# Two attention layers on one core: VectorE in written order for the first two attentions, and a last chunk with its own sums

## The chip, the cores and the metric

The kernel runs on one core of one Trainium2 chip. Its time is the device time of one execution in microseconds (us). Before the change the median of 9 runs is 3087.87 us (3086.91 to 3088.94). A profile of one execution stands beside it; this execution itself took 3088.43 us.

The engines of a core work side by side, each through its own list of instructions in order: TensorE (PE) multiplies matrices into PSUM, VectorE (DVE) and ScalarE (ACT) work on elements, GpSimd (POOL) does little here, and SyncE (SP) issues most DMAs. Semaphores order work between engines.

## The reference

The input `x` has 8 images of 64 channels and 64 x 64 positions (n = 4096). Two layers follow one another:

```python
# layer 0, for each image
f, g, hh = Wf @ x + bf, Wg @ x + bg, Wh @ x + bh     # 8, 8 and 64 channels
beta = softmax(f^T @ g)                              # 4096 x 4096
x = x + hh @ beta^T
# layer 1, for each image
xn = group_norm(x, 8 groups) * gamma + beta
q, k, v = split(w_qkv @ xn + b_qkv)                  # 64 channels each
o = softmax(q^T @ k / 8) @ v
out = x + w_proj @ o + b_proj
```

All of it is in float32.

## The kernel before

**Layout.** An image lies on 128 partitions: 64 channels times two halves of its positions, 2048 columns each. An attention is cut into NC = 4 chunks of 512 query columns per half (1024 queries), and a chunk into NT = 16 steps of keys. A step gives one tile `e` of 128 x 2048 float32, exponentials of scores for 256 keys and 1024 queries. There are six buffers of `e` (pool `ppool`, line 101).

**A step.** TensorE makes scores in PSUM banks, ScalarE writes their exponentials to `e` (line 877 for layer 0, line 836 for layer 1), TensorE multiplies `e` with the values and adds this up in a bank (`weigh`), and VectorE adds `e` to the running sum `esum` (line 749), which becomes the denominator of the softmax. There is no maximum subtracted; instead a flag `n_bad` counts sums outside a range, and if it isn't zero a general path (lines 894 on) does all again. With these inputs the general path does not run.

**Banks.** Of eight PSUM banks, 0 and 7 hold the weighted sums (`outer`), the six between are three pairs that `pair()` hands out in turn (`turn`, lines 110 to 120). In layer 0 a group of scores takes six or seven banks, and a projection borrows a pair (`lent`).

**End of a chunk.** `finish` (line 327) copies the weighted sum to `raw`, folds `esum`, and gives three pieces of work that are done some steps later: `sums` (products with ones, a copy to `zs`, four small DMAs to `zt`), `reciprocals` (a reciprocal into `stash` on 8 columns, then a DMA to DRAM and two that broadcast it to `r`) and `result` (multiply, residual). The very last chunk has a function of its own, `end` (line 379): it adds up the sums on VectorE, turns them to columns by eight products, takes the reciprocal on 128 x 8, tests the bounds, spreads the reciprocals by a diagonal matrix `diag` and two products, and writes the output over two queues.

**Order of the attentions.** It is layer 0 of image 0, layer 0 of image 1, layer 1 of image 0, layer 0 of image 2, layer 1 of image 1, and so on (lines 669 to 672). So only at the start do two attentions of layer 0 follow each other. While the second runs, the group norm and the projections of layer 1 of image 0 are made: `channels` (aggregate of the statistics), `means`, `deviations` (an inverse square root by four Newton rounds, 16 small operations) and `normal` (which makes `xn`), lines 552 to 614. In the same way the projections of the next attention of layer 0 (`project`, line 488: `full` on ScalarE, then `high` and its split on VectorE, then 16 DMAs) are made in steps of the one before.

**What sets the order.** Each piece of work is put down for a step with `at_step` and taken by `take` (line 685) in the loop over steps, between scores and weighing. The matmuls are chained in the order in which they are written (`in_order`, line 124, and `matmul`). The instructions of VectorE and ScalarE are not: a scheduler places them by its own estimate, and `issue_after` only holds some of them back. VectorE's list in the built program is therefore not the written one; small operations lie between the running sums.

Of the kernel before, what the change touches and what calls it, by code (L numbers as in the profile page):

```python
# [19 lines left out]
CW = 512  # L20
# [12 lines left out]
@with_exitstack  # L33
def kernel(
    ctx: ExitStack,
    tc: tile.TileContext,
    x: bass.AP,
    WfT: bass.AP,
    bf: bass.AP,
    WgT: bass.AP,  # L40
    bg: bass.AP,
    WhT: bass.AP,
    bh: bass.AP,
    gamma: bass.AP,
    beta: bass.AP,
    WqkvT: bass.AP,
    bqkv: bass.AP,
    WpT: bass.AP,
    bp: bass.AP,
    out: bass.AP,  # L50
):

    nc = tc.nc
    args = (x, WfT, bf, WgT, bg, WhT, bh, gamma, beta, WqkvT, bqkv, WpT, bp, out)
    flag = ctx.enter_context(tc.tile_pool(name="flag", bufs=1))  # L60
    n_bad = flag.tile([1, 1], I32, name="n_bad")
    fast_path(tc, n_bad, *args)
    reg = nc.values_load(n_bad[0:1, 0:1], min_val=0, max_val=2 * P)
    with tc.If(reg > 0):
        general_path(tc, *args)
# [3 lines left out]
def fast_path(  # L69
# [42 lines left out]
    turn = 0  # L112
# [9 lines left out]
    tensor_last = None  # L122

    def in_order(made):

        nonlocal tensor_last
        if tensor_last is not None:
            tc.add_manual_dep(
                made.ins,
                tensor_last.name,  # L130
                mybir.DependencyInfo(mybir.DependencyClass.NoSync, mybir.DependencyReason.DATA),
                reason="order",
            )
        tensor_last = made.ins
# [165 lines left out]
    class Attention:  # L300
# [8 lines left out]
        def values(self, src, w, c):  # L309
# [11 lines left out]
            copy = nc.vector.tensor_copy if lent is None or first_ else nc.scalar.copy  # L321
# [5 lines left out]
        def finish(self, acc, esum, c, index):  # L327
# [6 lines left out]
            with tc.issue_after(copied.ins if self.kind == 1 else added):  # L334
                nc.vector.tensor_add(esum[:, 0], esum[:, 0], esum[:, 1])  # L335
# [27 lines left out]
            def reciprocals():  # L363
                rt = stash[:, ts(index, QP)]
                nc.vector.reciprocal(rt, zt)
# [7 lines left out]
            def result():  # L373
                nc.vector.tensor_mul(raw, raw, r)  # L374
                self.residual(raw, c)
# [3 lines left out]
        def end(self, acc, esum, e, t):  # L379


            c = NC - 1
            total = esum[:, 0]
            with tc.issue_after(added):
                for part in (esum[:, 1], e[:, 0], e[:, 1]):
                    nc.vector.tensor_add(total, total, part)  # L386
            z, laid = pair()[:, 0, 0:QP], pair()[:, 0, :]
            parts = [(h, k) for h in range(2) for k in range(TPC)]
            for p in range(2):
                self.weigh(acc, e[:, p], t, p, False, p == 1, slice(0, CW))  # L390
            for i, (h, k) in enumerate(parts):
                matmul(
                    z[:, i : i + 1], total[:, h, ts(k, P)], ones[:, 0:1], start=True, stop=True
                )
            rt = small.tile([P, QP], F32, tag="zt", bufs=4, name="rt")
            nc.vector.reciprocal(rt, z)
            bounds(rt, 1)
            raw = work.tile([P, CW], F32, tag="raw", bufs=4, name="raw_end")
            diag = work.tile([P, QP, P], F32, tag="full", bufs=1, name="diag")
            for h in range(2):  # L400
                nc.vector.tensor_mul(  # L401
                    diag[:, ts(h, TPC), :],
                    ident.unsqueeze(1).broadcast_to([P, TPC, P]),
                    rt[:, ts(h, TPC)].unsqueeze(2).broadcast_to([P, TPC, P]),
                )
            self.total(raw, acc)
            for i in range(2):
                matmul(bad_ps, bad[:, i : i + 1], ones[:, 0:1], start=i == 0, stop=i == 1)
            nc.vector.tensor_copy(n_bad, bad_ps)
            for h in range(2):  # L410
                matmul(
                    laid[ts(h, C), :], ones, diag[:, ts(h, TPC), :].rearrange("q k n -> q (k n)"),
                    start=True, stop=True,
                )
            nc.vector.tensor_mul(raw, raw, laid)
            self.residual(raw, c, (nc.sync, nc.scalar))

    class Layer0(Attention):
# [51 lines left out]
        def project_direct(self):  # L470
# [4 lines left out]
            for i, dst in enumerate((self.f, self.g)):  # L475
# [6 lines left out]
                nc.vector.tensor_copy(high[:, i, :], full[:, i, :])  # L482
                nc.vector.scalar_tensor_tensor(
# [4 lines left out]
        def project(self, k, js=(0, 1)):  # L488
# [14 lines left out]
            nc.vector.tensor_copy(high[rows], full[rows])  # L503

            split = high
            self.split = nc.vector.scalar_tensor_tensor(  # L506
# [31 lines left out]
        def residual(self, o, c):  # L538
            xc = x_tiles[self.b][:, ts(c, CW)]
            nc.vector.scalar_tensor_tensor(xc, o, hb, xc, op0=ALU.add, op1=ALU.add)  # L540
            nc.vector.bn_stats(self.st[:, c, :], xc)

    class Layer1(Attention):
# [8 lines left out]
        def before(self):  # L552
# [7 lines left out]
            def channels():  # L560
                nc.vector.bn_aggr(mv, self.st())

            def means():
# [5 lines left out]
                nc.vector.tensor_sub(d, mv[:, 0:1], mu)  # L569
                nc.vector.scalar_tensor_tensor(v, d, d, mv[:, 1:2], op0=ALU.mult, op1=ALU.add)  # L570

            def deviations():
# [4 lines left out]
                nc.vector.tensor_scalar_add(ve, ve, EPS)  # L577

                guess = small.tile([P, 1], I32, tag="guess", name=f"guess_{n}")
                nc.vector.tensor_single_scalar(  # L580
                    guess, ve.bitcast(I32), 1, op=ALU.logical_shift_right
                )
                nc.vector.tensor_scalar(
# [4 lines left out]
                for i in range(4):  # L588
                    nc.vector.scalar_tensor_tensor(w, y, y, ve, op0=ALU.mult, op1=ALU.mult)  # L589
                    nc.vector.tensor_scalar(w, w, -0.5, 1.5, op0=ALU.mult, op1=ALU.add)  # L590
                    nc.vector.tensor_mul(y, y, w)
                nc.vector.tensor_mul(self.a, y, k1["gam"])

            def normal(c):
                xns[c] = work.tile([P, CW], F32, tag="xn", bufs=1, name=f"xn_{n}_{c}")
                nc.vector.tensor_scalar(  # L596
# [8 lines left out]
            at = [18, 21, 24] if self.b == 0 else [16, 20, 24]  # L605
            units = [(at[0], channels, False), (at[1], means, True), (at[2], deviations, True)]
            for c in range(NC):
                s = 30 + 8 * c
                units += [
                    (s - 3, lambda c=c: normal(c), False),  # L610
# [42 lines left out]
        def total(self, raw, acc):  # L653
            nc.vector.tensor_copy(raw, acc[0])  # L654
            return nc.vector.tensor_add(raw, acc[1], raw)

        def residual(self, o, c, queues=(nc.sync, nc.sync)):
            nc.vector.scalar_tensor_tensor(
                o, o, k1["pb"], x_tiles[self.b][:, ts(c, CW)], op0=ALU.add, op1=ALU.add
            )  # L660
            for h in range(2):
                queues[h].dma_start(out[self.b, :, ds(h * NH + c * CW, CW)], o[ts(h, C), :])
# [71 lines left out]
    def weigh(i, j, e, cols, now):  # L734
# [12 lines left out]
        else:  # L747
            with tc.issue_after(layers0[0].split.ins) if i == 0 and t == 1 else nullcontext():
                added = nc.vector.tensor_add(esum, first if t == 1 else esum, e).ins  # L749
# [56 lines left out]
    bad = const.tile([P, 2], F32, name="bad")  # L806
    bad_ps = banks[0:1, 0, 0:1]

    def bounds(recip, i):
        ok = work.tile(list(recip.shape), F32, tag="raw", bufs=4, name=f"ok_{i}")  # L810
        nc.vector.tensor_scalar(ok, recip, 1.0 / SUM_MAX, None, op0=ALU.is_ge)
        nc.vector.scalar_tensor_tensor(
            ok, recip, 1.0 / SUM_MIN, ok, op0=ALU.is_le, op1=ALU.mult
        )
        least = small.tile([P, 1], F32, tag="least", name=f"least_{i}")
        nc.vector.tensor_reduce(least, ok, axis=AX.X, op=ALU.min)
        nc.vector.tensor_scalar(bad[:, i : i + 1], least, -1.0, 1.0, op0=ALU.mult, op1=ALU.add)

    at_step(len(seq) * NT - 3, lambda: bounds(stash, 0), 0)

    i = 0
    while i < len(seq):
        at, c = seq[i]
        if at.kind == 1:
# [64 lines left out]
    assert not later  # L889
    seq[-1][0].end(acc, esum, ready[0][2], NT - 1)  # L890
# [387 lines left out]
```

## Time and profile before

| | us |
|---|---|
| median of 9 runs | 3087.87 |
| the profiled execution | 3088.43 |
| its span, first to last instruction | 3086.7 |
| TensorE busy | 3051.4 (99%) |
| VectorE busy | 2534.8 (82%) |
| ScalarE busy | 2043.7 (66%) |
| mean granted TensorE clock | 0.995 |
| one running sum (line 749), 895 of them | 2.291 each, 2050.2 in all |

A line of a group or of the timeline names the source line, the engine, the operation, the tile written, the tile read and their shapes; in brackets stands how long the engine was idle just before and what ended this idle time. A line of waits has the total in us, how often, and the longest. A line of windows has the stretch, its length, and then the busy time of TensorE, its weight loads, VectorE, ScalarE and GpSimd with their number of instructions, and after them the granted TensorE clock (1.00 is full speed), the share of busy DMA engines and GB/s. A float32 matmul stands in the trace as two records, so the counts of matmuls there are twice those of the code.

### The profile page before, as it was taken

How to read it: one execution, taken by the hardware profiler on the slowest of the kernel's cores; microseconds unless marked ns; L12 is line 12 of the kernel's file. 1: busy time of each engine (PE TensorE's matmuls, PEld its weight loads, DVE VectorE, ACT ScalarE, POOL GpSimd, SP SyncE). 2: the span in 40 equal slices, each digit the busy share in tenths (PEclk: the TensorE clock that was granted, in tenths of full speed). 3: DMA queues.
4: the chain of work that ended last, by engine and by line, in shares of the span. 5: the costliest groups of instructions: out<-in, count | busy, mean ns of one | idle time of the engine just before them, and what ended most of it. 6: DMA issues, size and time to landing. Idle time of an engine off the chain costs nothing.

```text
span 3086.7 us, 59407 instructions
## 1 busy us (share of the span) xinstructions
PE 3051.4 (99%) x26083; PEld 1134.3 (37%) x26083; DVE 2534.8 (82%) x1612; ACT 2043.7 (66%) x1999; POOL 16.9 (1%) x45
## 2 busy tenths in 40 slices
PE   8999999999999999999999999999999999999998
PEld 3333334333343333433334333343333433334433
DVE  7998877899768997689877898779987799876666
ACT  7877655786557865578655785558855588555554
POOL 2000000000000000000000000000000000000000
PEclk9999999999999999999999999999999999999999
DMA  3000010100101001010010100100001000000000
GB/s 78 22 8 11 18 39 15 32 1 15 39 18 29 1 15 39 22 25 1 15 39 22 25 1 18 41 21 22 1 26 35 19 8 1 15 22 15 9 15 12
DMA packets 57531, 62.54 MB, mean 20 GB/s; under 512 B 30816, under 2 KB 30864, under 8 KB 57264
## 3 DMA queue, kind: packets, MB, share of 16 engines
q1 hardware_dynamic: 56192, 58.38, 7.6%
q8 instruction: 206, 3.38, 0.5%
q14 instruction: 61, 0.50, 0.1%
q0 software_dynamic: 672, 0.12, 0.0%
q10 hardware_dynamic: 400, 0.17, 0.0%
HBM read 25.06 MB, written 8.65 MB: 11 GB/s over the span
## 4 chain that ended last, share of the span: by engine, by line
PE 93%; DVE 5%; issue 1%; ACT 1%; DMA 0%; SPq 0%; DVEq 0%; ACTq 0%
PE banks L137 93%; DVE esum_l L749 4%; ACT e_l L836 0%; ACT e_l L877 0%; DVE vt_l L322 0%; DVE esum_l L386 0%; DVE esum_l L335 0%; DMA x<-in_x_dram 0%; ACT full_l L501 0%; DVE x L540 0%; DVE raw_l L374 0%; SPq L166 0%; DVE high_l L506 0%; DVE diag L401 0%; DVE w_l L589 0%
## 5 line engine op out<-in xcount | busy, mean ns | idle before, releaser
L749 DVE TENSOR_TENSOR esum_l<-esum_l,e_l 128x2048 f32<-128x2048 f32 x895 | 2050.2, 2291 | 461.7 <-ACT e_l L836 403.6
L836 ACT ACTIVATE e_l<-banks 128x1024 f32<-128x1024 f32 x1024 | 992.9, 1022 | 800.1 <-PE banks L137 776.7
L137 PE MATMUL banks<-e_l,v_l 64*64 64x512 f32 (+2 forms) x8772 | 1104.1, 589 | 0.0
L877 ACT ACTIVATE e_l<-banks 128x2048 f32<-128x2048 f32 (+3 forms) x765 | 956.2, 1314 | 196.9 <-PE banks L137 189.8
L137 PE MATMUL banks<-kq_l 64*64 64x512 f32 (+1 forms) x8448 | 1009.8, 586 | 2.6 <-ACT e_l L877 1.3
L137 PE MATMUL banks<-e_l,vt_l 128*64 128x512 f32 (+1 forms) x4060 | 831.9, 550 | 0.0
L137 PEld LDWEIGHTS banks<-e_l,v_l 64*64 64x64 f32 (+1 forms) x8772 | 363.0, 134 | 577.1 <-issue 530.2
L137 PEld LDWEIGHTS banks<-kq_l 64*64 64x64 f32 (+1 forms) x8448 | 348.0, 135 | 577.9 <-issue 546.6
L137 PEld LDWEIGHTS banks<-e_l,vt_l 128*64 128x64 f32 x4060 | 266.9, 136 | 471.4 <-issue 451.3
L137 PE MATMUL banks<-fg_l 32*128 32x512 f32 x1792 | 209.4, 459 | 4.8 <-ACT e_l L877 3.2
L749 DVE TENSOR_TENSOR esum_l<-e_l,e_l 128x2048 f32<-128x2048 f32 x64 | 146.4, 2287 | 11.5 <-ACT e_l L836 9.4
L137 PEld LDWEIGHTS banks<-fg_l 32*128 32x128 f32 x1792 | 85.3, 182 | 187.2 <-ACT e_l L877 138.3
L335 DVE TENSOR_TENSOR esum_l<-esum_l 128x1024 f32<-128x1024 f32 x63 | 76.8, 1219 | 0.8
L654 DVE COPY raw_l<-banks 128x512 f32<-128x512 f32 x31 | 21.4, 691 | 31.3 <-PE banks L137 31.3
L628 ACT ACTIVATE kq_l<-banks,qkb 128x512 f32<-128x512 f32 x64 | 40.7, 697 | 4.0 <-PE banks L137 4.0
L374 DVE TENSOR_TENSOR raw_l<-raw_l,r_l 128x512 f32<-128x512 f32 x63 | 43.1, 684 | 0.0
L137 PE MATMUL banks<-esum_l,ones 128*32 128x256 f32 x504 | 40.3, 391 | 1.6 <-DVE vt_l L322 1.6
L137 PE MATMUL banks<-xn_l,wqk 64*64 64x512 f32 x256 | 34.3, 607 | 4.1 <-DVE xn_l L596 4.1
L137 PEld LDWEIGHTS banks<-wh,x 64*64 64x64 f32 x1024 | 23.1, 138 | 15.3 <-issue 14.2
L137 PEld LDWEIGHTS banks<-wvp,xn_l 64*64 64x64 f32 x1024 | 20.6, 134 | 16.8 <-issue 16.8
L536 ACT COPY raw_l<-banks 128x512 f32<-128x512 f32 x32 | 19.0, 593 | 11.6 <-PE banks L137 11.4
L540 DVE SCALAR_TENSOR_TENSOR x<-raw_l,hb,x 128x512 f32<-128x512 f32 x32 | 24.0, 751 | 1.1
(108 smaller groups left out, 392.0 us busy)
## 6 DMA issues: line engine op xcount, KB each, us to landing
r_l<-recips SPq DMA_DIRECT2D x126, 128.0 KB, 2.9
fg_l<-high_l SPq DMA_DIRECT2D x216, 64.0 KB, 2.0
kq_l<-kq_l SPq DMA_DIRECT2D x64, 128.0 KB, 2.3
out_dram<-raw_l SPq DMA_DIRECT2D x62, 128.0 KB, 2.4
x<-in_x_dram SPq DMA_DIRECT2D x30, 256.0 KB, 4.8
zt_l<-zs_l SPq DMA_DIRECT2D x252, 1.0 KB, 1.7
kq_l<-high_l SPq DMA_DIRECT2D x32, 64.0 KB, 2.0
recips<-stash SPq DMA_DIRECT2D x63, 4.0 KB, 1.4
```

Source lines behind the costliest of these rows:

```text
L137: in_order(nc.tensor.matmul(*args, **kwargs))
L335: nc.vector.tensor_add(esum[:, 0], esum[:, 0], esum[:, 1])
L374: nc.vector.tensor_mul(raw, raw, r)
L536: nc.scalar.copy(raw, acc[0])
L540: nc.vector.scalar_tensor_tensor(xc, o, hb, xc, op0=ALU.add, op1=ALU.add)
L628: nc.scalar.activation(self.parts[:, h, cols], ps[:, h, :], AF.Identity, bias=k1["qkb"][:, h : h + 1],)
L654: nc.vector.tensor_copy(raw, acc[0])
L749: added = nc.vector.tensor_add(esum, first if t == 1 else esum, e).ins
L836: nc.scalar.activation(e[:, p], both_ps[p], AF.Exp, scale=at.scale)
L877: nc.scalar.activation(e.rearrange("k p h n -> k (p h) n")[:, first_ : first_ + n_, :], banks[:, bank : bank + n_, :], AF.Exp, scale=at.scale,
```

## The change

- `in_order` now keeps a chain for each engine. All VectorE instructions of the fast path are made through `vector`, which adds them to VectorE's chain while `tight` is true: that is for the first two attentions (`i < 2 * NC`) and for `end`. In the rest, and in the units before the first step, VectorE's order is left to the scheduler as before.
- The unit numbers of layer 1 of image 0 move: `means` from 21 to 22, `deviations` from 24 to 26, the projections from 30 + 8c to 31 + 8c; `normal` is 4 steps ahead of its projection instead of 3, so its step stays (for other images it is one earlier than before).
- `turn` starts at 2 instead of 0.
- An `issue_after` at the first running sum is gone.
- `end` is written anew: the sums come from products with ones of the two halves of `esum` and of the sum of both halves of the last `e`, 12 products into one bank; the reciprocal is taken there on all 128 partitions, 4 groups of 32 equal rows, 256 columns; four products of 32 rows with a column of `ident` spread it; `raw` is copied by ScalarE. The flag is apart: `zs` is copied by ScalarE, dealt to 128 x 8 by two products, tested in two operations, and nine products of one column add it up. Both output DMAs go on SP.

The core of the diff:

```diff
-    turn = 0
+    turn = 2
...
+    made_last = {}
+    tight = False
+
+    def in_order(made, engine="tensor"):
...
+    class InOrder:
+        def __getattr__(self, name):
+            def made(*args, **kwargs):
+                it = getattr(nc.vector, name)(*args, **kwargs)
+                if tight:
+                    in_order(it, "vector")
+                return it
+
+            return made
+
+    vector = InOrder()
...
         def end(self, acc, esum, e, t):
             c = NC - 1
-            total = esum[:, 0]
-            with tc.issue_after(added):
-                for part in (esum[:, 1], e[:, 0], e[:, 1]):
-                    nc.vector.tensor_add(total, total, part)
-            z, laid = pair()[:, 0, 0:QP], pair()[:, 0, :]
-            parts = [(h, k) for h in range(2) for k in range(TPC)]
+            width = CW // 2
+            parts = [(h, i) for h in range(2) for i in range(2)]
+            groups = [slice(32 * g, 32 * (g + 1)) for g in range(4)]
+            ps, laid = pair(), pair()[:, :, 0:width]
+            z, dealt = ps[:, 0, 0:width], ps[:, 1, 0:QP]
+            both_e = ppool.tile([P, 2, 2, CW], F32, tag="e", name="both_e")[:, 0]
+            for k, src in enumerate((esum[:, 0], esum[:, 1], both_e)):
+                if k == 2:
+                    vector.tensor_add(both_e, e[:, 0], e[:, 1])
+                for rows, (h, i) in zip(groups, parts):
+                    matmul(
+                        z[rows, :], ones[:, 0:32], src[:, h, ts(i, width)],
+                        start=k == 0, stop=k == 2, tile_position=(0, rows.start),
+                    )
             for p in range(2):
                 self.weigh(acc, e[:, p], t, p, False, p == 1, slice(0, CW))
-            for i, (h, k) in enumerate(parts):
-                matmul(
-                    z[:, i : i + 1], total[:, h, ts(k, P)], ones[:, 0:1], start=True, stop=True
-                )
-            rt = small.tile([P, QP], F32, tag="zt", bufs=4, name="rt")
-            nc.vector.reciprocal(rt, z)
-            bounds(rt, 1)
-            raw = work.tile([P, CW], F32, tag="raw", bufs=4, name="raw_end")
-            diag = work.tile([P, QP, P], F32, tag="full", bufs=1, name="diag")
-            for h in range(2):
-                nc.vector.tensor_mul(
-                    diag[:, ts(h, TPC), :],
...
-                )
-            self.total(raw, acc)
-            for i in range(2):
-                matmul(bad_ps, bad[:, i : i + 1], ones[:, 0:1], start=i == 0, stop=i == 1)
-            nc.vector.tensor_copy(n_bad, bad_ps)
-            for h in range(2):
-                matmul(
-                    laid[ts(h, C), :], ones, diag[:, ts(h, TPC), :].rearrange("q k n -> q (k n)"),
-                    start=True, stop=True,
-                )
-            nc.vector.tensor_mul(raw, raw, laid)
-            self.residual(raw, c, (nc.sync, nc.scalar))
+            rt = work.tile([P, width], F32, tag="zs", name="rt")
+            vector.reciprocal(rt, z)
+            zs = work.tile([P, width], F32, tag="zs", name="zs_end")
+            nc.scalar.copy(zs, z)
+            raw = work.tile([P, CW], F32, tag="raw", bufs=4, name="raw_end")
+            nc.scalar.copy(raw, acc[0])
+            vector.tensor_add(raw, acc[1], raw)
+            for rows, (h, i) in zip(groups, parts):
+                matmul(
+                    laid[ts(h, C), i, :],
+                    ident[rows, rows.start : rows.start + 1].broadcast_to([32, C]), rt[rows, :],
+                    start=True, stop=True, tile_position=(rows.start, h * C),
+                )
+            by_half = raw.rearrange("p (i n) -> p i n", i=2)
+            vector.tensor_mul(by_half, by_half, laid)
+            for k in range(2):
+                matmul(
+                    dealt[:, ts(k, 4)], zs[:, ts(k, P)], ident[:, 0:P:32], start=True, stop=True
+                )
+            ok = small.tile([P, QP], F32, tag="zt", bufs=4, name="ok_end")
+            vector.tensor_scalar(ok, dealt, SUM_MIN, -1.0, op0=ALU.is_ge, op1=ALU.mult)
+            vector.scalar_tensor_tensor(
+                bad[:, 1:], dealt, SUM_MAX, ok, op0=ALU.is_le, op1=ALU.mult
+            )
+            for i in range(1 + QP):
+                matmul(bad_ps, bad[:, i : i + 1], ones[:, 0:1], start=i == 0, stop=i == QP)
+            nc.scalar.copy(n_bad, bad_ps)
+            self.residual(raw, c)
...
-            at = [18, 21, 24] if self.b == 0 else [16, 20, 24]
+            at = [18, 22, 26] if self.b == 0 else [16, 20, 24]
...
-                s = 30 + 8 * c
+                s = 31 + 8 * c if self.b == 0 else 30 + 8 * c
                 units += [
-                    (s - 3, lambda c=c: normal(c), False),
+                    (s - 4, lambda c=c: normal(c), False),
...
+        tight = i < 2 * NC
...
+    tight = True
     seq[-1][0].end(acc, esum, ready[0][2], NT - 1)
```

## The prediction

> **What bounds the kernel now.** I read the page first, then TensorE's waits, then the stretch in which they lie by windows, then the timeline of VectorE and ScalarE around it, and last the tail.
>
> ```profile
> PE 3051.4 (99%) x26083; PEld 1134.3 (37%) x26083; DVE 2534.8 (82%) x1612; ACT 2043.7 (66%) x1999; POOL 16.9 (1%) x45
> ```
>
> TensorE is busy in 99% of the span, so only its 35 us of idle time, and time at a low clock, can be won: no matmul of the two long phases is removed. TensorE's waits:
>
> ```profile
> PE banks L137 <- DMA x<-in_x_dram: 6.4, 1, 6.4
> PE banks L137 <- ACT e_l L877: 4.5, 8, 1.3
> PE banks L137 <- DVE xn_l L596: 4.1, 1, 4.1
> PE banks L137 <- DVE v_l L570: 2.8, 1, 2.8
> PE banks L137 <- DVE bad L817: 2.4, 1, 2.4
> ...
> PE banks L137 <- ACT mu_l L567: 1.2, 1, 1.2
> ```
>
> The single waits for `xn_l`, `v_l`, `mu_l` and `mv_l` (0.6) lie between 219 and 262 us, in the second attention, where the group norm of the first one is worked out. With 0.13 of an `e_l` wait they make 8.9 us. By windows (length, then PE busy; the column after POOL is the granted clock):
>
> ```profile
> 219.00:226.00 7.00, 5.06 (x35) 2.02 (x33) 6.89 (x5) 4.57 (x7) 0.00 (x0) 1.00 0.00 0
> 226.00:231.00 5.00, 5.00 (x24) 1.34 (x16) 4.79 (x3) 2.11 (x3) 0.00 (x0) 0.66 0.01 1
> 231.00:239.00 8.00, 5.18 (x21) 1.77 (x17) 7.65 (x7) 2.11 (x3) 0.00 (x0) 0.65 0.01 2
> 239.00:243.00 4.00, 4.00 (x23) 1.33 (x23) 3.90 (x6) 3.14 (x2) 0.00 (x0) 0.85 0.00 0
> 243.00:255.00 12.00, 8.22 (x51) 2.86 (x51) 11.64 (x18) 8.93 (x8) 0.00 (x0) 0.95 0.00 0
> 255.00:262.00 7.00, 6.66 (x29) 1.95 (x33) 2.49 (x2) 1.49 (x3) 0.00 (x0) 0.59 0.16 37
> ```
>
> Busy time times clock, summed, is 26.9 us of work in 43: 8.9 idle and 7.2 lost to the clock. But VectorE is busy all the while, and ScalarE already waits for it:
>
> ```profile
> 224.07 1.02 ACT L877 ACTIVATE e_l<-banks 128x1024 f32<-128x1024 f32 x1 [1.52 <-DVE esum_l L749]
> ...
> 255.20 2.28 DVE L749 TENSOR_TENSOR esum_l<-esum_l,e_l 128x2048 f32<-128x2048 f32 x1
> 262.84 2.29 DVE L749 TENSOR_TENSOR esum_l<-esum_l,e_l 128x2048 f32<-128x2048 f32 x1 [5.35 <-ACT e_l L877]
> ```
>
> `e` has six buffers, so the exponential of step t waits for the running sum of step t-6. VectorE runs without a gap from 26.9 to 257.5 us, at 2.40 us a sum, against about 2.25 for a step of TensorE: in these two attentions in a row it falls six tiles behind. Its 5.35 us of idle at 262.84 is the time it caught up while TensorE stood. So VectorE, not TensorE, says how much of the 16.1 us comes back.
>
> **The change, part 1: statistics earlier.** In the order of the built programs, the norm's aggregate, mean, deviation and the 16 small Newton operations no longer lie spread among the sums: all of them and the first `xn` now stand before sum 8 of chunk 1, where `xn` stood after sum 13. The unit numbers move deviations and projections by one or two steps. TensorE's bound alone would be +16.1 us. Now VectorE's clock in the new order (sum (c,t): chunk c, step t, of the second attention):
>
> - The split of `high_l` (0.69 + 1.28 us) of the second attention now stands after the first attention's sum 8 of chunk 0, not after sum 11.
>
> ```profile
> 46.05 7.08 DVE L749 TENSOR_TENSOR esum_l<-esum_l,e_l 128x2048 f32<-128x2048 f32 x3
> ...
> 46.99 1.12 ACT L501 ACTIVATE full_l<-banks,fgb_low 128x1024 f32<-128x1024 f32 x1
> ```
>
> Sum 8 ends at 45.95, but its input `full_l` is only made by 48.11: VectorE stands 2.2 us, with every later sum behind it. The 16 DMAs behind the split start earlier, at 50 instead of 55, which nobody waits for. The later split of chunk 1 (input at 88.19, slot at 89.4) and the reciprocals (`zt` landed at 80.3, slot at 84.6) do not wait.
> - Instructions on independent data overlap by 0.08 us; a sum behind a sum starts 0.10 after it, a small dependent one 0.04. Written order puts dependent ones together: counting the pairs, +0.38 (residual of chunk 0), +0.62 (of chunk 2) and +0.43 (of chunk 3, with the aggregate).
> - Sum (1,1) therefore ends at 223.98 + 2.2 + 1.43 = 227.6. Up to sum (1,9) come eight sums (18.7 with overlaps), two small (0.3), the Newton block (ve, two guesses, 12, gain: 3.2) and `xn` (0.5): 250.3.
> - The exponential of (1,15) may start then: its first half runs to 251.4, two `kq_l` copies (0.69 each) to 252.7, the scores behind them to 253.0. Before, the same scores ended at 261.96: 9.0 gained. Against it: 0.5, since 32 `wvp` products (0.7) now come one group later while two more scores are done; 0.4 at exponential (2,6), whose sum (2,1) ends at 268.6 where TensorE would be there at 268. Later steps of TensorE take 2.52 us (302.5 less 262.7 over 16) against VectorE's 2.4, so the gain stays.
>
> TensorE's new waits before 253 are short and cost nothing while VectorE has six tiles queued. If that cover is gone they cost their length, about 7 us. The mean's matmul waits longer than now (aggregate at 225.6, TensorE there at 224.3), and the `ve` copy on ScalarE (by 239.4, behind half an exponential) leaves VectorE, at its place at 239.7, only 0.3 us of room; each us late there is one us.
>
> [...] 0.58 and 1.23 us of wait close together were followed by 0.66. So many waits of 1 us, as I expect from 160 to 253, can cool it too. [...]
>
> **Part 2: `turn = 2`.** The pairs rotate from another start. The waits at the six turns of layer (0.41 and 0.27 us each) are alike in all three phases, so nothing there. At the start the third of the first four scores now falls into a bank whose reader `full_l` ends at 14.95, not into one that is free: these two scores and the exponential (14.97) come 0.5 later, the copy behind it waits until 17.06 for VectorE anyway, so 0.25 us lost.
>
> Part 1 and 2: 9.0 - 0.5 - 0.4 - 0.25 = **7.8 us**; bounds 2 (VectorE loses twice what I count, and a cold window) to 12.
>
> **Part 3: the tail.**
>
> ```profile
> 3068.03 3.61 PE L137 MATMUL banks<-e_l,v_l 64*64 64x512 f32 x32
> 3072.22 1.95 PE L137 MATMUL banks<-ones,esum_l 128*128 128x1 f32 x16 [0.58 <-DVE esum_l L386]
> ...
> 3080.32 0.52 ACTq L662 DMA_DIRECT2D out_dram<-raw_end  x1
> ```
>
> Removed: three adds in a row (1.22 each), eight column products (1.95), two `diag` products on VectorE (0.68 each), a copy, two 512-wide products (1.98, at half clock). New: 12 products for the sums (0.64 per four, from the same product in the chunks), one add of both e halves (1.22), a reciprocal 128x256, ScalarE copies (0.38, 0.59), 4 + 2 + 9 small products.
>
> TensorE: old products to 3069.9, 8 sum products to 3071.1, four more to 3071.7 (the add, 3069.4 to 3070.6, is hidden), last weighing to 3073.6. Reciprocal from 3071.8. Its length is unknown: the row has 0.20 us for 8 columns against 0.15 for one column of another operation, so between 0.46 ([...] at the rate of the sums, 2.29 us for 2048) and 1.8 (the 0.05 us as 6.6 ns a column). [...] I take 1.8, the row's steep reading. The copy `zs` waits for it and the copy of `acc` for `zs`, so above 1.0 each us costs one. Then: `zs` 3073.6 to 3074.0, `raw` 3074.6, add 3075.4, multiply 3076.1, two flag operations 3076.4, residual 3077.1; it ended at 3080.28. Flag: nine products 0.7, copy 0.2: 3077.3, where `n_bad` stood at 3077.33. Both output DMAs now go on SP, the second 0.6 later: landed by 3080.7 (3083.27 before).
>
> The end is ScalarE's now: in the records of its sequencer the DMA issue (to 3080.83), a load of the flag (1.2), the branch, 3.5 us until the next instruction at 3085.70, 0.95 to the end. Without the DMA ScalarE loads from 3077.35, and its branch is over by 3081.8 to 3082.1; TensorE's (3.8 us) ends at 3081.8 as now. So 3085.7 - 3081.8 = **4.0 us** rounded up, [...] 4.6 with 0.46; below, 0.5 if the flag's chain or the branches stretch.
>
> Sum: 7.8 + 4.0 = 11.8. The profiled execution took 3088.43 for a span of 3086.7, so 3076.6; against the median of 3087.87 it is **3076.1 us**.
>
> **Rivals.**
> - A: written order hurts VectorE more: head waits at `ve`, the aggregate and the split. The 0.3 us of room speaks for it, six queued tiles against. Part 1 gives 1.5: 3082.4.
> - B: the tail's gain is lost to the flag chain and the far branches, 0.5 kept. Speaking for it: TensorE's 3.8 us. 3087.9 - 7.8 - 0.5 = 3079.6.
> - C: VectorE's lag is smaller than I count (the split finds its input, overlaps stay): part 1 gives 12: 3071.9.
> - D, slower: the clock. From 100 to 262 TensorE has 145 us of work at full clock. With a share c of this time at half rate it takes 145/(1 - c/2): c is 0.1 now, the tail's 4 us are gone at c = 0.27, and at 0.35 it is 176 instead of 162: 3087.9 + 14 - 4 = 3098. Against it: a lone 1.27 us wait at 186 left the clock at 1.00.
>
> **How the numbers follow.** Forecast 0.58, A 0.17, B 0.10, C 0.10, D 0.05. A measurement of this kernel can tell about 0.2%, 6.2 us. Faster: the forecast, B and C, and a third of A: 0.84. Same: the rest of A: 0.12. Slower: 0.04. The forecast's own range is 3073.5 to 3079.5; from 3071.5 (C) to 3083 (A) leaves under 2 in 10 out.
>
> **What would show it.** After: no TensorE wait for `xn_l` or `v_l`; VectorE idle of about 2 us before `high_l` near 46; waits of TensorE for `e_l` from about 100 to 253; the scores of 261.96 at about 253; VectorE without its 5.35 us gap. In the tail the residual at 3077 less 7.8 and ScalarE's branch without a DMA ahead. Wrong it would be if VectorE's idle between 27 and 250 exceeds 4 us, or the clock falls below 0.8 from 100 to 250.

## The result and the profile after

The changed kernel takes 3077.1 us (median of 9 runs, 3075.9 to 3078.2) where the kernel before takes 3087.8 (29 runs beside it): a ratio of 0.9965, with a 95% interval of 0.9957 to 0.9974. The forecast was 3076.1. The profiled execution took 3076.42 us for a span of 3074.6, against 3088.43 for 3086.7.

The busy times of the page, and TensorE's waits, longest sums first:

```profile
PE 3046.7 (99%) x26113; PEld 1133.1 (37%) x26113; DVE 2533.3 (82%) x1604; ACT 2045.3 (67%) x2004; POOL 16.6 (1%) x45
```

```profile
PE banks L150 <- ACT e_l L902: 7.3, 12, 1.1
PE banks L150 <- DMA x<-in_x_dram: 6.3, 1, 6.3
...
PE banks L150 <- DVE mv_l L140: 1.4, 1, 1.4
PE banks L150 <- DVE bad L140: 1.4, 1, 1.4
```

TensorE's waits for `xn_l` (4.1), `v_l` (2.8) and `mu_l` (1.2) are gone. Those for `e_l` rose from 4.5 to 7.3, and the one for `mv_l` from 0.6 to 1.4: a part of the old idle time has moved to where VectorE holds TensorE back through the six `e` buffers. (`L140` is now the line of the helper that makes every VectorE instruction, so go by the tiles.)

The windows of the stretch where the gain was to come from (length, busy TensorE, weight loads, VectorE, ScalarE, GpSimd, then the granted clock):

```profile
219.00:226.00 7.00, 4.48 (x27) 1.76 (x27) 6.86 (x6) 4.47 (x4) 0.00 (x0) 1.00 0.00 0
226.00:231.00 5.00, 5.00 (x26) 1.59 (x26) 4.86 (x5) 1.71 (x4) 0.00 (x0) 0.66 0.00 0
231.00:239.00 8.00, 8.00 (x45) 2.77 (x43) 7.83 (x4) 6.50 (x7) 0.00 (x0) 1.00 0.02 3
239.00:243.00 4.00, 4.00 (x29) 1.57 (x27) 2.90 (x15) 3.19 (x4) 0.00 (x0) 1.00 0.00 0
243.00:253.00 10.00, 10.00 (x62) 3.33 (x58) 9.79 (x8) 8.24 (x10) 0.00 (x0) 1.00 0.00 0
```

From 231 on TensorE has no gap and the full clock; before, it was busy in 24.1 of the 31 us from 231 to 262, at a mean clock of 0.78. Ahead of it little has changed: 2.5 us of idle from 219 to 226 where it was 1.9, and then the same mean clock of 0.66, from one stretch at half clock. VectorE around these places:

```profile
48.04 0.69 DVE L140 CAST high_l<-full_l 128x1024 fp32r<-128x1024 f32 x1 [2.13 <-ACT full_l L526]
...
240.24 0.15 DVE L140 TENSOR_SCALAR ve_l<-ve_l 128x1 f32<-128x1 f32 x1 [0.65 <-ACT ve_l L601]
...
245.64 0.54 DVE L140 TENSOR_SCALAR xn_l<-x,mu_l,a_l 128x512 f32<-128x512 f32 x1
```

The first exponential of chunk 2 of the second attention, my marker below for the end of this stretch, is the second of the two in each of these rows, after and before:

```profile
252.99 2.79 ACT L902 ACTIVATE e_l<-banks 128x1024 f32<-128x1024 f32 x2
```

```profile
261.78 2.37 ACT L877 ACTIVATE e_l<-banks 128x1024 f32<-128x1024 f32 x2 [3.13 <-PE banks L137]
```

It starts at 253.91 (262.70 before): 8.8 us. At later points the same 8.7 us stand between the two traces (479.63 and 470.89, 2475.28 and 2466.54), so after 254 nothing is won or lost until the last chunk. There VectorE's list is:

```profile
3057.24 2.29 DVE L140 TENSOR_TENSOR esum_l<-esum_l,e_l 128x2048 f32<-128x2048 f32 x1 [1.14 <-ACT e_l L861]
3060.68 1.22 DVE L140 TENSOR_TENSOR both_e<-e_l 128x1024 f32<-128x1024 f32 x1 [1.14 <-ACT e_l L861]
3062.71 1.76 DVE L140 RECIPROCAL rt<-banks 128x256 f32<-128x256 f32 x1 [0.81 <-PE banks L150]
...
3067.07 0.74 DVE L140 SCALAR_TENSOR_TENSOR raw_end<-raw_end,pb,x 128x512 f32<-128x512 f32 x1
```

From the end of the last running sum (3059.53) to the end of the span it is 15.1 us, where it was 18.4 (3068.24 to 3086.65).

### The profile page after: what moved, and what is told of

It reads as the page before. It is cut to its first block, busy times and chain, and to the rows that moved or that the text cites. A ratio compares the mean times of both kernels' runs of the same rounds, so it can differ in the third digit from the quotient of the medians.

```text
span 3074.6 us, 59457 instructions
## 1 busy us (share of the span) xinstructions
PE 3046.7 (99%) x26113; PEld 1133.1 (37%) x26113; DVE 2533.3 (82%) x1604; ACT 2045.3 (67%) x2004; POOL 16.6 (1%) x45
## 4 chain that ended last, share of the span: by engine, by line
PE 94%; DVE 4%; ACT 1%; issue 1%; DMA 0%; SPq 0%; DVEq 0%; ACTq 0%
PE banks L150 94%; DVE esum_l L140 3%; ACT e_l L902 0%; ACT e_l L861 0%; DVE vt_l L140 0%; DMA x<-in_x_dram 0%; ACT full_l L526 0%; DVE rt L140 0%; DVE w_l L140 0%; DVE x L140 0%; SPq L179 0%; DVE raw_l L140 0%; DVE raw_end L140 0%; DVE st_l L140 0%; DVE guess_l L140 0%
## 5 line engine op out<-in xcount | busy, mean ns | idle before, releaser
L140 DVE TENSOR_TENSOR esum_l<-esum_l,e_l 128x2048 f32<-128x2048 f32 x895 | 2050.2, 2291 | 453.3 <-ACT e_l L861 403.6
L902 ACT ACTIVATE e_l<-banks 128x512 f32<-128x512 f32 (+3 forms) x767 | 957.0, 1311 | 193.6 <-PE banks L150 177.8
L140 DVE TENSOR_TENSOR esum_l<-e_l,e_l 128x2048 f32<-128x2048 f32 x64 | 146.3, 2286 | 6.5 <-ACT e_l L861 6.5
L140 DVE TENSOR_TENSOR esum_l<-esum_l 128x1024 f32<-128x1024 f32 x63 | 76.9, 1220 | 0.9
L140 DVE COPY raw_l<-banks 128x512 f32<-128x512 f32 x31 | 21.4, 691 | 31.3 <-PE banks L150 31.3
L140 DVE TENSOR_TENSOR raw_l<-raw_l,r_l 128x512 f32<-128x512 f32 x63 | 43.1, 684 | 0.0
L150 PEld LDWEIGHTS banks<-wh,x 64*64 64x64 f32 x1024 | 23.0, 137 | 14.9 <-issue 13.9
L140 DVE SCALAR_TENSOR_TENSOR x<-raw_l,hb,x 128x512 f32<-128x512 f32 x32 | 24.0, 751 | 1.1
```

Of the source, the lines that this page charges most:

```text
L140: it = getattr(nc.vector, name)(*args, **kwargs)
L150: in_order(nc.tensor.matmul(*args, **kwargs))
L902: nc.scalar.activation(e.rearrange("k p h n -> k (p h) n")[:, first_ : first_ + n_, :], banks[:, bank : bank + n_, :], AF.Exp, scale=at.scale,
```

## The experiments

My theory after reading this trace: from 27 to 253 us VectorE is the limit, so each us it stands still there is a us of the time. Rivals: the unit numbers carry the gain; TensorE's waits for `e_l` have another cause; the two halves of the change share a gain. Differences to the kernel before are taken on the same chip. The changed kernel was measured beside its variants only in the last group (changed_again); elsewhere a difference to its 3077.1 goes across chips, on which the kernel before has medians from 3087.5 to 3088.3.

**The front alone, the last chunk alone, and the front without written order**

```diff
 front_only: the old end(), bounds() and two output queues in the changed kernel
 tail_only: the new end() and bounds() in the kernel before
 scheduler_order, in the changed kernel:
-        tight = i < 2 * NC
+        tight = False
 old_units, in the changed kernel:
-            at = [18, 22, 26] if self.b == 0 else [16, 20, 24]
+            at = [18, 21, 24] if self.b == 0 else [16, 20, 24]
-                s = 31 + 8 * c if self.b == 0 else 30 + 8 * c
+                s = 30 + 8 * c
-                    (s - 4, lambda c=c: normal(c), False),
+                    (s - 3, lambda c=c: normal(c), False),
```

> The changed kernel with the old last chunk (three adds, diagonal matrix, output over two queues): only the order of VectorE, the unit numbers and the turn are new. My theory: the two parts lie in different stretches and add up; the front gives 8.7 us, so 3079.1 us, and the first exponential of chunk 2 of the second attention starts at 253.9 as in the changed kernel (262.7 before). Rival (the new last chunk and the front share a gain, for instance through the bank rotation at the end): the front alone gives 10 to 12 us, 3076 to 3078, or under 7.

> The kernel before with the new last chunk alone. My theory: 3.3 us, so 3084.5 us; from the end of the last running sum to the end of the span 15.1 us instead of 18.4. The prediction's own figure: 4.0 us, 3083.8. Rival B of the prediction (flag chain and branches eat it): 0.5 us, 3087.3.

> The changed kernel, but VectorE's order in the first two attentions is left to the scheduler; the new unit numbers and the new last chunk stay. In the built program the Newton operations are then spread over the sums 9 to 13 of chunk 1 and the first normalised tile stands after sum 14. My theory (written order carries the front's gain): VectorE reaches that tile about 2.4 us later than before the change, TensorE's projection comes one step (2.25) later, so the front gives 0, between -1 and +2.5 us: 3084.5 us, 3082 to 3086; TensorE waits about 4 us for xn_l, and not for v_l. Rival (the unit numbers carry it, since they give VectorE time): 3077 to 3079, no wait for xn_l.

> The changed kernel with written order, but with the old unit numbers (mean 21, deviations 24, projections 30 + 8c, normalised tile 3 steps ahead). My theory (VectorE's order carries the gain; it stands before its sums whichever step TensorE's part has): the variance is ready at 230.3 and TensorE's product comes at 233, the normalised tile at 246.2 and TensorE at 246.6, so no new long wait; VectorE, which is the limit, does the same work: 3077.1 us, +0.5 at most, the first exponential of chunk 2 at 253.9 plus or minus 0.5. Rival (the unit numbers are needed): waits of TensorE for v_l or xn_l of 2 to 5 us together, 3079 to 3082.

| | median us | ratio to before, 95% |
|---|---|---|
| before | 3087.47 | |
| front_only | 3080.37 | 0.9978 (0.9970 to 0.9987) |
| tail_only | 3083.88 | 0.9989 (0.9981 to 0.9997) |
| scheduler_order | 3086.97 | 1.0000 (0.9991 to 1.0008) |
| old_units | 3077.61 | 0.9969 (0.9957 to 0.9981) |

The front gives 7.1 us and the last chunk 3.6; together 10.7, which is the whole change. They add up, as far as intervals of some 2.6 us to either side can tell; which part of the new last chunk gives its share was not taken apart. But the front's 7.1 was expected as 8.7, and its marker stands at 255.69 instead of 253.9: a miss that the next table explains.

With the order left to the scheduler the front's gain is not only gone, the front is some 3 us slower than before (3086.97 against 3083.88 of tail_only; the ranges do not touch). TensorE's waits in that run:

```profile
PE banks L150 <- DVE xn_l L140: 12.8, 1, 12.8
...
PE banks L150 <- DMA fg_l<-high_l: 2.0, 1, 2.0
```

The direction was as I expected, the size not: I had a wait of 4 us for `xn_l`, and it is 12.8. With the wait for `v_l` gone TensorE runs on to the projection and meets all of VectorE's lag in one place. The scheduler has spread the Newton operations over the sums, as it did in the kernel before:

```profile
247.08 2.29 DVE L140 TENSOR_TENSOR esum_l<-esum_l,e_l 128x2048 f32<-128x2048 f32 x1
249.29 0.15 DVE L140 TENSOR_TENSOR guess_l<-guess_l,w_l 128x1 f32<-128x1 f32 x1
...
252.64 2.29 DVE L140 TENSOR_TENSOR esum_l<-esum_l,e_l 128x2048 f32<-128x2048 f32 x1
254.85 0.15 DVE L140 TENSOR_TENSOR guess_l<-guess_l,w_l 128x1 f32<-128x1 f32 x1
...
257.95 0.54 DVE L140 TENSOR_SCALAR xn_l<-x,mu_l,a_l 128x512 f32<-128x512 f32 x1
```

Five sums of 2.29 us stand in and behind this chain of 16 operations of 0.15 to 0.22 us, and `xn_l` comes at 258.0, behind sum 14 of chunk 1, where written order makes it at 245.6, behind sum 7.

The 3 us by which this run is slower than tail_only point to another place. The dropped `issue_after` kept the first running sum behind the second split of image 0. Without it the scheduler puts sums ahead of this split and into it, TensorE waits 2.0 us for the split's DMAs (`fg_l`, at 34.5 us), and VectorE later stands:

```profile
43.41 2.29 DVE L140 TENSOR_TENSOR esum_l<-esum_l,e_l 128x2048 f32<-128x2048 f32 x1 [2.58 <-ACT e_l L902]
46.53 7.09 DVE L140 TENSOR_TENSOR esum_l<-esum_l,e_l 128x2048 f32<-128x2048 f32 x3 [0.83 <-ACT e_l L902]
```

These 3.4 us of idle are of the right size; they were not tried apart. So this run shows what all of the written order is worth, the start included, and not the Newton chain's part alone. The old unit numbers with written order, on the other hand, cost nothing (3077.61, and no wait for `v_l` or `xn_l`). So written order carries the front's gain, and with it the unit numbers add none that can be measured.

**What VectorE's idle time is worth**

```diff
 split_later: VectorE's part of the second attention's first projection one step later
+                at_step(now + 2, spread, 0)   # high_l, its split, the 16 DMAs
 three_sums_less:
+            if i == NC and t in (5, 6, 7):
+                return
             added = vector.tensor_add(esum, first if t == 1 else esum, e).ins
 turn_zero:
-    turn = 2
+    turn = 0
 output_on_scalar, the last chunk's second half:
-                nc.sync.dma_start(out[self.b, ...], o[ts(h, C), :])
+                (nc.scalar if last and h else nc.sync).dma_start(out[self.b, ...], o[ts(h, C), :])
```

> The changed kernel, but VectorE's part of the second attention's first projection (high_l, its split and their DMAs) is written one step later, behind sum 9 of chunk 0 instead of sum 8, when its input is there; nothing else moves. My theory (VectorE is the limit from about 27 to 253 us): its idle of 2.1 us before high_l goes, and with it 2.1 us of the time: first exponential of chunk 2 at 251.8 us instead of 253.9, 3075.0 us (between 3074.8 and 3075.9, the latter if the later wait for ve_l grows). Rival (TensorE's waits for e_l have another cause, such as banks or ScalarE): 253.9 and 3077.1.

> The changed kernel without the running sums of steps 5, 6 and 7 of chunk 0 of the second attention (so these tiles are missing in that chunk's softmax sums): 7.2 us less work for VectorE at about 200 us, nothing else changed. My theory: TensorE's waits that lie behind that place go (1.1 for e_l at 224 us, 1.4 for mv_l at 226, and the 1.7 us that the low clock costs between 226 and 231), so 4.2 us and no more, since the waits before 195 us (3.0) stay: first exponential of chunk 2 at 249.7 us, 3072.9 us. Rival (VectorE is not the limit): 253.9, 3077.1. Second rival (TensorE has no other bound near): the full 7.2 us, 246.7, 3069.9.

> The changed kernel with turn = 0 as before. My theory: the waits of TensorE at the six turns of layer stay 0.41 and 0.27 us, the start is 0.25 us shorter: 3076.8 us, not to be told from 3077.1. Rival (the rotation matters for the front or for the last chunk's banks): more than 1 us either way, seen as a new wait of TensorE for a pair of banks.

> The changed kernel with the second output DMA of the last chunk on ScalarE instead of SP. My theory (the end is set by SP, behind the landing of its second DMA): from the end of the last running sum to the end of the span 13.9 us instead of 15.1, so 3075.9 us. Rival, the prediction's reading (the far branches of ScalarE and TensorE set the end, and a DMA ahead of ScalarE's branch delays it): 15.1 to 15.6, 3077.1 to 3077.6.

> The changed kernel once more, for a comparison with the next three on the same chip. My theory: the time from high_l's start to the first exponential of chunk 2 is 205.2 us plus VectorE's wait for ve_l (0 to 2 us, by how long the clock stays at half after TensorE's two waits at 224 and 226 us); median 3077.1 us. Rival (that sum is not constant): it differs from 205.2 plus that wait by more than 0.3 us.

Medians: 3077.04 for split_later (0.9963, 0.9949 to 0.9977), 3072.58 for three_sums_less (0.9950, 0.9935 to 0.9965), 3077.99 for turn_zero (0.9966, 0.9953 to 0.9979), 3077.35 for output_on_scalar (0.9965, 0.9952 to 0.9979), 3076.83 for changed_again (0.9965, 0.9951 to 0.9978). By the medians, moving the split gave nothing, and the theory looks refuted. The traces say otherwise. Two things vary from one execution to the next: how long TensorE's clock stays at half in its first steps, and whether it falls to half again near 225 us. The second, for the changed kernel, for the same kernel again, and for turn_zero:

```profile
222.57:225.98 3.41, 0.89 (x9) 0.56 (x9) 3.38 (x4) 2.89 (x3) 0.00 (x0) 1.00 0.00 0
225.98:229.39 3.41, 3.41 (x12) 1.16 (x12) 3.31 (x2) 1.17 (x3) 0.00 (x0) 0.50 0.00 0
229.39:232.81 3.42, 3.42 (x26) 1.08 (x24) 3.35 (x5) 2.37 (x2) 0.00 (x0) 1.00 0.00 0
```

```profile
222.22:225.63 3.41, 2.09 (x13) 0.66 (x9) 3.27 (x3) 2.15 (x2) 0.00 (x0) 1.00 0.00 0
225.63:229.04 3.41, 2.20 (x14) 1.07 (x14) 3.31 (x4) 1.77 (x3) 0.00 (x0) 1.00 0.00 0
```

```profile
221.97:225.38 3.41, 1.64 (x11) 0.52 (x7) 3.27 (x3) 2.62 (x3) 0.00 (x0) 1.00 0.00 0
225.38:228.79 3.41, 2.66 (x10) 1.50 (x12) 3.31 (x4) 1.77 (x2) 0.00 (x0) 0.50 0.00 0
228.79:232.21 3.42, 3.42 (x12) 0.73 (x8) 3.38 (x4) 0.80 (x3) 0.00 (x0) 0.50 0.00 0
```

In all three TensorE waits 1.1 and then 1.4 to 1.5 us there (for `e_l` and `mv_l`), and yet the clock is at half for 3.4 us, not at all, and for 6.8 us. The windows are cut at whole steps of 3.413 us from a change of the clock: in each of the 14 traces all changes of the clock lie on one grid with this step, to within 0.01 us (in the changed kernel at 14.35, 21.18, 225.98, 229.39 and 3069.28 us), and the place of the grid differs from one execution to the next (it has a border at 225.98, 225.63 and 225.38 us in these three). In the changed kernel both waits fall into one step, TensorE is busy for 0.89 of its 3.41 us, and the next step is at half clock. In changed_again a border of the grid cuts the second wait, 2.09 and 2.20 us stay busy, and the clock holds. In turn_zero the first step has 1.64 busy, the rest of the second wait lies in the step at half clock, and one more follows.

The start hangs on the same grid. In the changed kernel the half clock of the first steps ends at 21.2 us and the third tile's exponential starts at 22.85; in changed_again it ends at 24.2, and the exponential, which waits for TensorE in both, starts at 24.05. Over the runs this start lies between 22.85 and 24.14 us, and `high_l` of the second attention, which waits for `full_l`, follows 25.2 us later in all seven runs of the table below.

In four of the five runs of the table below with half clock near 225 us, TensorE was then late with the product for `ve_l`, and VectorE stood for 0.65 to 2.02 us at that place, behind which all its sums are queued:

```profile
237.81 2.29 DVE L140 TENSOR_TENSOR esum_l<-esum_l,e_l 128x2048 f32<-128x2048 f32 x1
241.92 0.15 DVE L140 TENSOR_SCALAR ve_l<-ve_l 128x1 f32<-128x1 f32 x1 [1.82 <-ACT ve_l L601]
```

(turn_zero; the changed kernel's wait of 0.65 is shown above.) Put side by side:

| run | idle before high_l | high_l starts | at half clock, 221 to 260 us | VectorE's wait for ve_l | marker | marker less high_l's start less that wait |
|---|---|---|---|---|---|---|
| changed kernel | 2.13 | 48.04 | 3.41 | 0.65 | 253.91 | 205.22 |
| changed_again | 3.98 | 49.23 | 0 | 0 | 254.39 | 205.16 |
| front_only | 3.69 | 48.70 | 6.83 | 1.73 | 255.69 | 205.26 |
| turn_zero | 3.50 | 48.53 | 6.83 | 1.82 | 255.60 | 205.25 |
| output_on_scalar | 3.60 | 48.33 | 0 | 0 | 253.48 | 205.15 |
| old_units | 2.93 | 48.86 | 3.41 | 0 | 254.23 | 205.37 |
| split_later | 1.77 | 49.29 | 6.83 | 2.02 | 255.71 | 204.40 |

The last column is VectorE's time between the two points (a wait of 0.46 us near 203 us, which all seven have, is in it). It is the same within 0.1 us in the five runs that have VectorE's order of the changed kernel, however TensorE's clock stood. So VectorE is the limit, us for us. In split_later it is 0.8 less: one sum of 2.3 now stands ahead of `high_l`, and waits of 0.53 (`wvt`) and 0.90 (`full_l` of chunk 1) that were hidden show up behind it, which leaves 0.87. Its profiled execution had the latest start but one, and the longest wait for `ve_l`. I had expected 2.1 us by leaving the later waits out, and the median does not tell even 0.87 from nothing.

three_sums_less leaves three tiles out of that chunk's denominators, so it does not compute the attention; it shows the other side. Its median is 4.5 us under the changed kernel's 3077.1, with 4.2 expected, not 7.2. From the third tile's exponential to the marker it takes 226.4 (24.14 to 250.56) where the changed kernel takes 231.1 (changed_again 230.3). VectorE then stands for TensorE and DMAs at `zt_l` (1.72), `mu_l` (0.79) and `ve_l` (0.94), so with 7 us less work VectorE is no longer the limit throughout.

turn_zero: its first exponential starts at 14.46, 1 us earlier than the changed kernel's (but first_sum_early, with `turn = 2`, has 14.49), but the third tile is back in the range of the others (23.35). The waits at the turns of layer are as they were. The 0.9 us of its median are within what its wait for `ve_l` does; of `turn` nothing can be told.

output_on_scalar: from the last running sum's end to the end of the span it is 14.7 us instead of 15.1, in one trace; nine others with the new last chunk lie between 14.8 and 15.3, and the median shows no gain. Expected were 13.9 by my theory and 15.1 to 15.6 by the rival; neither is right. In the changed kernel SP waits until 3072.38 for the second output DMA (issued at 3068.36) and then works through some 20 semaphores to 3073.72. TensorE's next instruction after its far branch comes at 3072.64. Take the DMA away from SP, and SP waits for ScalarE and VectorE, whose branches are over at 3072.8, although this trace's last running sum ended 0.4 us earlier. Of the 1.2 us that I expected 0.4 came at most, since the branches stand right behind the landing.

**Taking VectorE's idle time away for good**

```diff
 splits_apart:
+            def spread():            # high_l, split and DMAs of project(), as before
...
+            if apart:                # 4 for the second attention's first half, 3 for its second
+                at_step(now + apart, spread, 0)
...
+            units = [(at[0], channels, False), (at[1], means, True), (at[2] - (self.b == 0), deviations, True)]
+            if self.b == 0:
+                units.append((at[2], lambda: newton(made["ve"]), False))
 first_sum_early, in addition:
+                self.project(1, apart=4, then=loads)    # image 0: sum 1 ahead of its second split
 all_together, in addition: the flag's two operations ahead of the multiply in end(),
 and the output as in output_on_scalar
```

> The changed kernel with VectorE's parts that wait for another engine written later: both splits of the second attention's projections three and two sums later, and ve_l's product one step earlier with the Newton operations at their place. My theory (VectorE's idle between 27 and 253 us is the loss): no idle over 0.5 us before high_l and ve_l, first exponential of chunk 2 at 251.1 us, whatever the start; 3074.0 us, between 3073.3 and 3074.8. Rival (moving the split alone gave no gain in the median, so these waits cost nothing): 3077.1.

> The run before this one, and in addition the first running sum ahead of the first image's second split: VectorE then does it in the 8 us in which it stood before 24.9 us. My theory: VectorE is another 2.3 us ahead at 27 us and still the limit at 253: first exponential of chunk 2 at 248.8 us, 3071.9 us, between 3071 and 3073. Rival (TensorE has become the limit, or the later split makes it wait for fg_l): no gain over the run before, 3074.0 or more.

> The run before this one, with the flag's two operations ahead of the multiply in the last chunk and the second output DMA on ScalarE. My theory (at the end the far branches and SP's landing come within 0.8 us of each other, so both have to be moved): from the end of the last running sum to the end of the span 14.4 us instead of 15.1, 3071.2 us in all. Rival (the end hangs on the residual's operation, which is now 0.35 us later): 15.1 to 15.4.

| same chip | median us | range | ratio to before, 95% | marker |
|---|---|---|---|---|
| changed_again | 3076.83 | 3076.18 to 3078.65 | 0.9965 (0.9951 to 0.9978) | 254.39 |
| splits_apart | 3073.56 | 3072.98 to 3073.88 | 0.9953 (0.9939 to 0.9966) | 251.37 |
| first_sum_early | 3072.59 | 3072.35 to 3073.24 | 0.9951 (0.9937 to 0.9964) | 249.74 |
| all_together | 3072.06 | 3071.93 to 3072.43 | 0.9949 (0.9935 to 0.9962) | 251.60 |

VectorE's two places in splits_apart now have no idle time ahead of them:

```profile
53.15 0.69 DVE L140 CAST high_l<-full_l 128x1024 fp32r<-128x1024 f32 x1
...
237.63 0.15 DVE L140 TENSOR_SCALAR ve_l<-ve_l 128x1 f32<-128x1 f32 x1
```

Its marker stands at 251.37 (251.1 expected), although its third tile started 0.7 us later than in the changed kernel's first trace (23.59) and its clock was at half for 3.41 us near 225: neither reaches VectorE any more. The range of its times is 0.9 us where that of changed_again is 2.5. In first_sum_early VectorE does a sum in the hole before 24 us:

```profile
19.31 2.29 DVE L140 TENSOR_TENSOR esum_l<-e_l,e_l 128x2048 f32<-128x2048 f32 x1 [3.21 <-ACT e_l L922]
23.80 0.69 DVE L140 CAST high_l<-full_l 128x1024 fp32r<-128x1024 f32 x1 [2.20 <-DMA fg_l<-high_l]
```

In the changed kernel that second row has 8.18 us of idle ahead of it, and the sum comes after the split. The gain is 1.0 us instead of 2.1 (the ranges of the two runs overlap): VectorE is now far enough ahead to wait for `zt_l` (1.31 at 80 us). all_together shortens the last chunk to 14.1 us (14.4 expected), 1 us less than the changed kernel, of which the median shows 0.5, with ranges that overlap; in its profiled execution the clock was at half for 6.83 us near 225, and the scores, not VectorE, came late (marker 251.60). Each of the three is faster than both kernels, all_together by 4.8 us against changed_again, and their ranges do not touch it.

## Why the prediction came out right, step by step

- **VectorE as the limit** holds, and the table above and splits_apart show it. Sum (1,1) ended at 227.62 and was put at 227.6; the aggregate at 225.48 (225.6), sum (1,9) at 250.70 (250.3), the `kq_l` copies at 253.00 (252.7).
- **The split's stall of 2.2 us** was 2.13 in the first profile, but 3.5 to 4.0 in four other runs of the same order. I took the start of one execution of the old kernel for the start of the new one. This agreement was partly luck. My own sign of being wrong, more than 4 us of idle time on VectorE between 27 and 250 us, stayed away in the first profile (3.2) but came in output_on_scalar (4.1), changed_again (4.4), turn_zero (5.8) and front_only (5.9).
- **The 0.3 us of room at ve_l** was the step that failed. I wrote that TensorE's new waits before 253 "are short and cost nothing while VectorE has six tiles queued", and that each us late at `ve_l` is one us. The second half is right. The first is not: in five of the seven executions of the table half clock followed the wait for `e_l` and the mean's wait, for 3.41 or 6.83 us, and VectorE's wait for `ve_l` was 0 to 2.02 us in these five.
- **The deductions** of 0.5 (`wvp`), 0.4 (exponential (2,6)) and 0.25 (`turn`) did not show. The front gave 8.74 in the profiled execution against 7.8, and 7.1 in the median of front_only. The size came out right because two errors went opposite ways, which is luck. (One step of the working is off: 302.5 less 262.7 over 16 is 2.49, not 2.52; it stays above VectorE's 2.4, so nothing hangs on it.)
- **The clock.** By the row (0.58 and 1.23 us of wait, then 0.66) I let it fall after short waits, and it did: in the changed kernel the waits of 1.07 and 1.44 us were followed by 3.41 us at half clock, in changed_again waits of 1.1 and 1.5 were not. The grid above corrects my reading of the row: of its two waits only the one of 1.23 lies in the step ahead of the half clock (223.13 to 226.55, TensorE busy in 2.19 us), the 0.58 lies in the step before. From 100 to 262 us, in all 14 traces, steps at full clock with a busy share up to 0.55 were followed by half clock and those from 0.58 on were not, but for this one with 0.64. So in these traces the half clock goes with the busy share of one step and not with the length of one wait, and so with where the grid happens to fall. A cold window, as in my bounds, costs 1.7 us by the row (5.00 us at 0.66). Rival D, a clock cold for long, did not come (by its own sum the last chunk's 4 us would be gone at a share of 0.25, not 0.27).
- **The last chunk.** The reciprocal took 1.76 us; I had taken 1.8 by the row. The residual ended at 3067.81, with the front's 8.7 added 3076.5, so 0.6 us earlier than forecast, and the flag's copy 0.7 earlier. Still the gain was 3.3 us in the trace and 3.6 in the median instead of 4.0. The failing term is the end itself: I had both DMAs "landed by 3080.7" and then nothing of SP's. The second landed at 3081.1 on that scale, and SP's closing semaphores (1.3 us), which ran in the shadow of ScalarE's branch before, came after it. In tail_only the second DMA landed early enough, SP waited for the branches again, and that trace gives 3.6 us.
- **The rivals.** A's head waits (split, `ve_l`) are real, but at prices that I had counted in part; its 3082.4 did not come. B falls with tail_only (3.6 us, not 0.5). C, that VectorE's waits are absent, is what splits_apart makes true, and it gives 3.3 us more.

## What to carry to other kernels

In the first two attentions VectorE took 2.40 us a sum against about 2.25 for a step of TensorE, and with the six buffers between them full each wait of its own cost its length (the last column of the table stays at 205.2 us, within 0.1, in five runs), though the page shows it busy for 82%. In such a place look for the slower engine's idle time, and write what it waits for later or earlier. Keep a chain of tiny dependent operations together in that engine's list: in scheduler_order five sums of 2.29 us in and behind such a chain brought `xn_l` at 258.0 us, in written order it came at 245.6. Where two traces of the same code differ (the marker at 253.91 and 254.39 us here), subtract the start and the clock before reading an effect of a us or two.

## What the runs showed of the hardware that I had not expected

- In the 14 traces the clock changed only at steps of 3.41 us (3.413 between neighbours), on a grid whose place differs by execution. Half clock lasted one to four steps ahead of the last chunk: 3.41, 6.83, 10.24 (first steps of changed_again, split_later and three_sums_less) and 13.65 us (from within the wait of 12.8 in scheduler_order). It ended after steps in which TensorE was busy for 0.88 to 1.00, and went on after some with up to 0.93.
- Of two output DMAs of 128 KB in a row on SP's queue, the first landed 2.5 us after its issue and the second 4.0 in the changed kernel (3.9 to 4.2 in all nine traces with this last chunk in written order and both DMAs on SP), while in tail_only the median of both is 2.3. In the changed kernel the second is issued 0.2 us ahead of the end of ScalarE's branch instruction, in tail_only 1.2 us ahead; whether the branches delay it is not shown. The changed kernel and tail_only:

```profile
out_dram<-raw_end SPq DMA_DIRECT2D x2, 128.0 KB, 3.2
```

```profile
out_dram<-raw_end SPq DMA_DIRECT2D x2, 128.0 KB, 2.3
```

- After the branch over the general path the next instruction comes 3.3 us (ScalarE) to 4.0 us (TensorE) later, much as before the change (3.5 and 3.8). From the flag's copy (3067.93) to TensorE's return (3072.64) it is 4.7 us, and 4.7 too in output_on_scalar, where an output DMA was moved. In all_together, with the flag earlier, the copy stands 7.6 us behind the last running sum instead of 8.4.
